# Four graph layers on one core: the last output stage written in place of the nodes' own term, with row scaling moved from GpSimd to VectorE in its second half

## The chip, the cores and the metric

The kernel runs on one core of a Trainium2 chip. The metric is device time in microseconds (us): the median of several runs of the whole program. A core has five engines that run their own instruction streams side by side and wait for each other by semaphores: PE (TensorE, matrix products), DVE (VectorE), ACT (ScalarE), POOL (GpSimd) and SP (SyncE, which here only issues DMAs). In the profile, a name with a q, such as SPq or POOLq, is the queue of that engine: what its sequencer handles itself.

## The reference, cut to what matters

Four layers on a graph of 4096 nodes with 128 features each. `x` is 4096x128 and `adj` a sparse 4096x4096 matrix, all in fp32. Each layer is added to its input and then normalized over the features:

```
x = _layernorm(x + _L0_gnn_ref(x, adj, adj, W, a))      # signed attention
x = _layernorm(x + _L1_gnn_ref(x, adj, W0, b0, W1, b1)) # Chebyshev, two steps
x = _layernorm(x + _L2_gnn_ref(x, adj, weight, ...))    # attention, 4 heads
x = _layernorm(x + _L3_gnn_ref(x, adj, W_self, W_neigh))
```

The change lies in the last layer, whose core is

```
deg = jnp.clip(jnp.sum(adj, axis=1, keepdims=True), 1.0)
h_neigh = adj @ h / deg
return h @ W_self + h_neigh @ W_neigh
```

with `h` the result of the third layer.

## The kernel before, in words

Nodes are cut into 32 tiles of 128 (`NT`), and into 8 blocks of 512 (`NB`, with `TB` = 4 tiles each). Layers 0 and 1 stream `adj` in chunks of 512x512. While they do, lists of each node's neighbours are built; with them layer 2 gathers single rows instead of multiplying whole matrices (`gathers`, `edges`, `sums`, `divide`). All this is built by `network(True)`. A flag, found while the lists are built, says whether they hold all neighbours; if not, the general `network(False)` runs after it. Both stand in one program: at line 1952 a conditional reads the flag, and each engine branches past the second network when it has done its part of the first. After that comes the end of the program (recorded at line 1983), where each engine drains and they meet in a barrier.

Layer 3 follows layer 2 tile by tile. `layer3_rows` keeps two things for each tile of nodes: `y`, its term for the neighbours, and `x[:, t, :]`, the nodes' own term (`h @ W_self` and the residual, scaled). A column of ones in `y` makes the same product yield the row sums of `adj`. `layer3_product` multiplies `y` with columns of `adj` and `add_up` adds the products into `acc3`, which lies transposed, features by nodes.

`layer3_end` closes one block of 512 nodes, and is a generator of three parts:

- Part 1. PE turns the block's columns of `acc3` upright with the help of the identity and adds the product of the last tile into the same PSUM buffer `p` (lines 1796 and 1798). DVE makes the reciprocal degrees (1800, 1801). It then forms, for each of four tiles, `p` times the reciprocal plus `x` into `o`, with the row sum beside it (1803). Line 1805 fills the last feature with minus that sum, so that each row has mean zero. DVE also takes the square sum of tile 3 (1807).
- Part 2. ACT takes the square sums of tiles 0 to 2 (1811) and the square root for all four (1812).
- Part 3. DVE makes the reciprocal (1814). ACT scales the rows of tiles 0 and 1 (1818), POOL those of tiles 2 and 3 (1820). SP stores the block, 256 KB (1821).

`o` has three buffers in the pool `l2`; `x` is one tile for all 4096 nodes that lives through the whole kernel. For PE, DVE, ACT and POOL the order of the instructions is the one in which they are written in `sparse_layers`. The loop at its end interleaves the blocks:

```
for ib in range(NB + 1):
    if ib < NB:
        ends.append(layer3_end(NT - 1, 1, ib, late[ib // TB][:, ib % TB]))
        next(ends[-1])                # part 1 of block ib
    if ib:
        next(ends.popleft(), None)    # part 3 of block ib - 1
    if ib < NB:
        next(ends[-1])                # part 2 of block ib
```

On DVE, therefore, the order is part 1 of block n, line 1814 of block n-1, part 1 of block n+1; on ACT the scalings of block n-1, then the squares and the root of block n.

Of the kernel before, what the change touches and what calls it, by code (L numbers as in the profile page):

```python
# [11 lines left out]
F32 = mybir.dt.float32  # L12
# [5 lines left out]
ALU = mybir.AluOpType  # L18
# [3 lines left out]
P = 128  # L22
IB = 512
TB = IB // P
# [21 lines left out]
def adj_resnorm_d4(ctx: ExitStack, tc: tile.TileContext, x_in, xT_in, adj, adjT, pairs, w0g, w0gT, a0, w1a, b1a,  # L46
# [7 lines left out]
    nc = tc.nc  # L54
    N, F = x_in.shape
    NT = N // P
    NB = N // IB
# [15 lines left out]
    x = state.tile([P, NT, F], F32, name="x")  # L73
# [1501 lines left out]
    def sparse_layers(enter, lists, w, h0T):  # L1575
        psum, ps_p, ps_x = [enter(name=n, bufs=b, space=PSUM) for n, b in (("ps_u", 2), ("ps_p", 4), ("ps_x", 2))]
        l2 = enter(name="l2", bufs=2)
# [210 lines left out]
        def layer3_end(t0, n, ib, a):  # L1788


            p = ps_p.tile([P, TB, F], F32, name="pp")
            o = l2.tile([P, TB, F], F32, name="o", bufs=3)
            s = small.tile([P, 2, TB], F32, name="less", bufs=3)
            for k in range(TB):
                at = slice(ib * IB + k * P, ib * IB + (k + 1) * P)
                nc.tensor.matmul(p[:, k, :], acc3[:, at], ident, start=True, stop=False)
                for r in range(n):
                    nc.tensor.matmul(p[:, k, :], a[:, r, k * P:(k + 1) * P], y[:, t0 + r, :], start=False, stop=r == n - 1)
            r = small.tile([P, TB], F32, name="rdeg")
            nc.vector.tensor_scalar_max(r, p[:, :, F - 1], 1.0)  # L1800
            nc.vector.reciprocal(r, r)
            for k in range(TB):
                nc.vector.scalar_tensor_tensor(o[:, k, 0:F - 1], p[:, k, 0:F - 1], r[:, k:k + 1], x[:, ib * TB + k, 0:F - 1],  # L1803
                                               op0=ALU.mult, op1=ALU.add, accum_out=s[:, 0, k:k + 1])
            nc.vector.tensor_scalar_mul(o[:, :, F - 1], s[:, 0, :], -1.0)  # L1805
            junk = [l2.tile([P, F], F32, name=f"z{k}") for k in range(2)]
            nc.vector.scalar_tensor_tensor(junk[1], o[:, 3, :], 1.0, o[:, 3, :], op0=ALU.mult, op1=ALU.mult,  # L1807
                                           accum_out=s[:, 1, 3:4])
            yield
            for k in range(3):  # L1810
                nc.scalar.activation(junk[0], o[:, k, :], AF.Square, accum_out=s[:, 1, k:k + 1])  # L1811
            nc.scalar.activation(s[:, 1, :], s[:, 1, :], AF.Sqrt, bias=eps, scale=1.0 / F)
            yield
            nc.vector.reciprocal(s[:, 1, :], s[:, 1, :])  # L1814
            for k in range(TB):
                scale = s[:, 1, k:k + 1]
                if k < 2:
                    nc.scalar.activation(o[:, k, :], o[:, k, :], AF.Copy, scale=scale)  # L1818
                else:
                    nc.gpsimd.tensor_scalar(o[:, k, :], o[:, k, :], scale, None, op0=ALU.mult)  # L1820
            nc.sync.dma_start(out[ib * IB:(ib + 1) * IB, :].rearrange("(k p) f -> p k f", p=P), o)

        with tc.manual_schedule(engines={mybir.EngineType.PE, mybir.EngineType.DVE, mybir.EngineType.Activation,
# [56 lines left out]
            for ib in range(NB):  # L1880
                if ib in LAST:
                    continue
                p = ps_p.tile([P, IB], F32, name="pp")
# [58 lines left out]
# [3 lines that stand above are left out]
                    next(ends[-1])  # L1945
                if ib:
                    next(ends.popleft(), None)
                if ib < NB:
                    next(ends[-1])
# [37 lines left out]
```

## Time and profile before

| what | value |
|---|---|
| runs | 1702.2, 1701.87 and 1694.86 us; median 1701.87 |
| profiled execution, its own time | 1874.19 us |
| its span, first to last instruction | 1872.1 us |
| busy share of the span | PE 84%, DVE 58%, ACT 20%, POOL 40% |
| granted TensorE clock, mean | 0.912 |
| output stage (layer3_end, 8 blocks) | 1831.4 to 1860.3 us of the span |
| busy in 1846.7 to 1860.3 | PE 0, DVE 6.18, ACT 9.04, POOL 5.91 us |
| busy in 1860.3 to 1872.1 | no engine |

The profile is of one execution, and its times count from the start of its span. The busy shares are means over stages with different limits, so a stage is read by itself: in which order its instructions start, and what ended the idle time ahead of each. Instructions that only move registers, branch, wait or drain are not counted as busy; where no engine is busy they are found under their line, on the queue of their engine.

### The profile page before, as it was taken

Reading aid. Unit: us, or ns where it says so; the run is one execution under the profiler, and the core shown is the slowest. Engines: PE = TensorE matmul, PEld = TensorE weight load, DVE = VectorE, ACT = ScalarE, POOL = GpSimd, SP = SyncE. Lnnn points to the kernel's source line nnn. Section 1 sums busy time; section 2 is a strip of 40 time slices with the busy share of each in tenths; the row PEclk is TensorE's granted clock in tenths of the full one; section 3 lists DMA queues with packets and bytes.
Section 4 is the critical chain, followed back from the end, with each engine's and each line's share of the span. In section 5 each row is a group of like instructions: output and inputs, shape, how many; then the busy total and the mean of one; then the engine's idle time right before and its main releaser. Section 6 shows DMA issues by size and latency. Waiting matters only on the chain. (4 is left out here: it accounts for less than half of the span.)

```text
span 1872.1 us, 16259 instructions
## 1 busy us (share of the span) xinstructions
PE 1565.8 (84%) x4804; PEld 748.6 (40%) x4808; DVE 1089.5 (58%) x3185; ACT 371.7 (20%) x681; POOL 742.0 (40%) x1142
## 2 busy tenths in 40 slices
PE   6999999999999789789898986849934668867784
PEld 3344445444444334334344443424422334433433
DVE  5655457988798485865686211424344645546564
ACT  4765400100001010102000000212222101112123
POOL 0000000000001718260687878870057776766732
PEclk9999999999999999899898998979957788888897
DMA  9887665688887375666686865727844465666572
GB/s 373 338 323 278 230 242 193 255 311 307 293 298 263 113 265 171 255 210 226 216 280 241 279 248 193 267 73 261 261 103 138 149 227 184 213 210 225 187 205 68
DMA packets 102601, 429.24 MB, mean 229 GB/s; under 512 B 20387, under 2 KB 38822, under 8 KB 60646
## 3 DMA queue, kind: packets, MB, share of 16 engines
q1 hardware_dynamic: 64400, 380.99, 57.1%
q0 software_dynamic: 20352, 31.44, 6.7%
q10 hardware_dynamic: 17750, 15.67, 2.6%
q8 instruction: 40, 0.66, 0.1%
q14 instruction: 59, 0.48, 0.1%
HBM read 416.43 MB, written 11.60 MB: 229 GB/s over the span
## 5 line engine op out<-in xcount | busy, mean ns | idle before, releaser
L1666 POOL DMA_INDIRECT got<-table,source x288 | 276.3, 959 | 188.7 <-DVE most L1507 115.5
L1773 PE MATMUL pp<-chunk,xT 128*128 128x512 f32 x496 | 257.5, 662 | 5.5 <-issue 5.2
L1439 POOL DMA_INDIRECT both_ways<-in_pairs,both_at x108 | 107.7, 997 | 359.1 <-DVE both_at L1421 307.4
L691 PE MATMUL pacc<-chunk,t 128*128 128x512 f32 x512 | 227.8, 599 | 5.1 <-issue 3.9
L1439 POOL DMA_INDIRECT got<-rows,source x180 | 180.9, 1005 | 114.9 <-issue 95.8
L691 PE MATMUL pacc<-chunk,x 128*128 128x512 f32 x512 | 222.0, 592 | 0.0
L1319 DVE MAX8 top<-chunk 128x8 f32<-128x512 f32 x224 | 144.6, 679 | 86.1 <-DMA chunk<-in_adjT 81.6
L397 PE MATMUL pacc<-chunk,hw 128*128 128x512 f32 x408 | 186.8, 602 | 0.3 <-DVE hw L440 0.2
L1887 PE MATMUL pp<-chunk,w 128*128 128x512 f32 x384 | 183.2, 627 | 3.3 <-issue 3.3
L1320 DVE FIND_INDEX8 at<-top,chunk 128x8 uint16<-128x512 f32 x224 | 151.3, 685 | 0.0
L691 PEld LDWEIGHTS pacc<-chunk,t 128*128 128x128 f32 x512 | 96.6, 192 | 121.7 <-issue 119.7
L691 PE MATMUL pacc<-chunk,v 128*128 128x512 f32 x320 | 145.1, 604 | 0.0
L691 PEld LDWEIGHTS pacc<-chunk,x 128*128 128x128 f32 x512 | 96.3, 190 | 116.2 <-issue 116.2
L1773 PEld LDWEIGHTS pp<-chunk,xT 128*128 128x128 f32 x496 | 99.4, 214 | 97.5 <-issue 94.6
L1286 POOL IOTA i<- 128x384 int32 (+3 forms) x4 | 1.0, 259 | 336.7 <-PE pden L385 323.5
L397 PEld LDWEIGHTS pacc<-chunk,hw 128*128 128x128 f32 x408 | 74.3, 190 | 90.5 <-issue 85.6
L1887 PEld LDWEIGHTS pp<-chunk,w 128*128 128x128 f32 x384 | 75.2, 203 | 88.0 <-issue 88.0
L328 DVE TENSOR_SCALAR pos<-chunk 128x2048 bf16<-128x2048 f32 x66 | 80.4, 1222 | 43.7 <-DMA chunk<-in_adjT 42.3
L369 ACT ACTIVATE junk<-chunk 128x2048 fp8e4<-128x2048 f32 x51 | 97.4, 1910 | 27.2 <-DMA chunk<-in_adjT 26.6
L1483 POOL TENSOR_TENSOR idle<-idle 128x1 f32<-128x1 f32 x417 | 93.7, 225 | 7.0
L1786 DVE TENSOR_TENSOR acc<-pp,acc 128x512 f32<-128x512 f32 x96 | 62.2, 683 | 58.0 <-PE pp L1773 29.2
L1476 DVE SCALAR_TENSOR_TENSOR here<-got,back,here 128x128 f32<-128x128 f32 x120 | 42.1, 351 | 87.4 <-DMA got<-rows,source 75.9
(349 smaller groups left out, 1894.2 us busy)
## 6 DMA issues: line engine op xcount, KB each, us to landing
chunk<-in_adjT SPq DMA_DIRECT2D x346, 1024.0 KB
keep<-in_adjT SPq DMA_DIRECT2D x13, 1024.0 KB
spread<-spread ACTq DMA_DIRECT2D x16, 384.0 KB
got<-table,source POOLq DMA_INDIRECT x288
got<-rows,source POOLq DMA_INDIRECT x180
table<-rows ACTq DMA_DIRECT2D x8, 264.0 KB
xT<-in_xT ACTq DMA_DIRECT2D x8, 256.0 KB
rows<-v ACTq DMA_DIRECT2D x8, 256.0 KB
```

Of the source, the lines that this page charges most:

```text
L328: r = nc.vector.tensor_scalar(pos, a, 0.0, None, op0=ALU.is_gt)
L369: nc.scalar.activation(junk, a, AF.Relu, scale=-1.0, accum_out=bad[:, n:n + 1], saturate=False)
L397: in_order(nc.tensor.matmul(p, hw[:, j * TB + k, :], a[:, k, :], start=first and k == 0, stop=last and k == TB - 1))
L691: nc.tensor.matmul(p, stationary(c * TB + k), a[:, k, :], start=n == 0 and k == 0, stop=n == NB - 1 and k == TB - 1)
L1319: nc.vector.max(self.top[:, t, ib, :], row)
L1320: nc.vector.max_index(self.at[:, t, ib, :], self.top[:, t, ib, :], row)
L1439: tc.keep_in_program_order(nc.gpsimd.indirect_dma_start(out, None, of, bass.IndirectOffsetOnAxis(ap=index, axis=0)))
L1483: return nc.gpsimd.tensor_tensor(self.idle[:, 0:1], of, self.idle[:, 1:2], ALU.mult)
L1666: nc.gpsimd.indirect_dma_start(got[t][:, j, :], None, table, bass.IndirectOffsetOnAxis(ap=lists.source[:, t, j:j + 1], axis=0))
L1773: nc.tensor.matmul(p, y[:, t0 + k, :], a[:, ib % (TB // n), k, :], start=k == 0, stop=k == n - 1)
L1786: nc.vector.tensor_add(acc3[:, blk], p, acc3[:, blk])
L1887: nc.tensor.matmul(p, w[:, c * TB + k, :], a[:, k, :], start=n == 0 and k == 0, stop=n == NB - 1 and k == TB - 1)
```

## The change

The tile `o` no longer has buffers of its own: it names the block's four tiles of `x`, and line 1803 reads the nodes' own term from the place that it writes. In blocks 0 to 3 POOL scales the rows of tiles 2 and 3 as before. In blocks 4 to 7 one DVE instruction scales both, with the two reciprocals spread over 128 elements each. ACT's share, the order of the parts and the store are unchanged in the text.

```
-            o = l2.tile([P, TB, F], F32, name="o", bufs=3)
+            o = x[:, ib * TB:(ib + 1) * TB, :]
...
             for k in range(TB):
-                nc.vector.scalar_tensor_tensor(o[:, k, 0:F - 1], p[:, k, 0:F - 1], r[:, k:k + 1], x[:, ib * TB + k, 0:F - 1],
+                nc.vector.scalar_tensor_tensor(o[:, k, 0:F - 1], p[:, k, 0:F - 1], r[:, k:k + 1], o[:, k, 0:F - 1],
                                                op0=ALU.mult, op1=ALU.add, accum_out=s[:, 0, k:k + 1])
...
                 if k < 2:
                     nc.scalar.activation(o[:, k, :], o[:, k, :], AF.Copy, scale=scale)
-                else:
+                elif ib < NB // 2:
                     nc.gpsimd.tensor_scalar(o[:, k, :], o[:, k, :], scale, None, op0=ALU.mult)
+            if ib >= NB // 2:
+                nc.vector.tensor_tensor(o[:, 2:4, :], o[:, 2:4, :], s[:, 1, 2:4][:, :, None].to_broadcast([P, 2, F]), ALU.mult)
             nc.sync.dma_start(out[ib * IB:(ib + 1) * IB, :].rearrange("(k p) f -> p k f", p=P), o)
```

## The prediction

> **What bounds the kernel now.** The page first: no engine is full over the span (PE 84%, DVE 58%, POOL 40%), but the diff touches only `layer3_end`, the output stage, so shares of the whole span decide nothing here. The windows view puts that stage at 1831.4 to 1860.3 of 1872.1 us, with nothing busy after it. Next I read its timeline by engine. The columns are start, duration, engine, line and what it does; in brackets stand the idle time before it and who ended it.
>
> ```profile
> 1840.61 0.18 DVE L1814 RECIPROCAL less<-less 128x4 f32<-128x4 f32 x1 [0.24 <-ACT less L1812]
> ...
> 1842.60 0.35 DVE L1803 SCALAR_TENSOR_TENSOR o<-pp,rdeg,x 128x127 f32<-128x127 f32 x1 [1.55 <-DMA out<-o]
> ...
> 1844.23 0.17 DVE L1814 RECIPROCAL less<-less 128x4 f32<-128x4 f32 x1
> ...
> 1848.17 0.35 DVE L1803 SCALAR_TENSOR_TENSOR o<-pp,rdeg,x 128x127 f32<-128x127 f32 x1 [1.08 <-POOL o L1820]
> ...
> 1851.25 0.35 DVE L1803 SCALAR_TENSOR_TENSOR o<-pp,rdeg,x 128x127 f32<-128x127 f32 x1 [1.02 <-DMA out<-o]
> ...
> 1854.31 0.35 DVE L1803 SCALAR_TENSOR_TENSOR o<-pp,rdeg,x 128x127 f32<-128x127 f32 x1 [0.99 <-DMA out<-o]
> ...
> 1858.36 0.18 DVE L1814 RECIPROCAL less<-less 128x4 f32<-128x4 f32 x1 [2.25 <-ACT less L1812]
> 1858.57 0.69 ACT L1818 ACTIVATE o<-o,less 128x128 f32<-128x128 f32 x2 [0.24 <-DVE less L1814]
> 1858.69 1.18 POOL L1820 TENSOR_SCALAR o<-o,less 128x128 f32<-128x128 f32 x2 [1.24 <-issue]
> ```
>
> Four times L1803 stands still because its buffer of `o` (three exist) has not been stored yet; the one put down to POOL (whose work on that buffer was done at 1845.68) ends 2.5 us after that block's store was issued, so it is a store too. The last block closes with POOL's two scalings, 0.6 us behind ScalarE's.
>
> Then the part with no busy engine, from the answers on the lines of the conditional (L1952) and of the end of the program (L1983). The columns are queue, operation and count, duration in ns (least/median/most), first and last start.
>
> ```profile
> L1952 POOLq COMPARE_BRANCH  x1: 57/57/57, 1859.4 to 1859.4; - x1
> L1952 SPq COMPARE_BRANCH  x1: 58/58/58, 1860.3 to 1860.3; - x1
> ...
> L1952 POOLq EVENT_SEMAPHORE  x1: 17/17/17, 1862.5 to 1862.5; - x1
> ...
> L1983 POOLq DRAIN  x3: 40/107/8734, 1862.5 to 1871.8; - x3
> L1983 SPq DRAIN  x3: 7/7/13, 1864.8 to 1871.5; - x3
> ```
>
> Of POOL's three drains the first begins at 1862.5 and must be the long one: the next POOL record is at 1871.3. SP is through its own work at 1864.8 and waits about 6.5 us for the barrier. **The span ends on POOL's drain**, 0.9 us after it. So two things bound the end: the output blocks' chain, and after it the engine that was used last.
>
> [...] so I read the 8.73 us as execution, not as a wait for SP. [...] POOL's next record comes 3.1 us after its branch (1859.4 to 1862.5). [...]
>
> **The change, part by part.** Starts of L1814, one per block: 1838.18, 1840.61, 1844.23, 1846.65, 1849.80, 1852.88, 1855.93, 1858.36. Undisturbed steps are 2.43 us: ScalarE's round of two scalings (0.60 until the next may start), three squares with accumulator reads (1.3), a square root (0.30), and the way over L1814 and back. The steps with a stall are 3.62, 3.15, 3.08 and 3.05, so the stalls cost 1.19 + 0.72 + 0.65 + 0.62 = 3.18 us.
>
> 1. *Output in place.* The buffer wait goes: a block of `x` is written once and stored once, and no later block reuses it. The instructions and their shapes stay. In-place output costs nothing: L1786 already adds in place at 683 ns mean, 692 in this window. All eight steps become 2.43 us: **-3.2 us**. Late next is ScalarE's round; the products are not, since PE ends at 1845.9, ahead of the last blocks.
> 2. *Blocks 4 to 7: two POOL instructions become one DVE instruction.* [...] L1632, 128x264, 432 ns at the median. It starts when L1814 is done, 0.21 us after that one's start, while L1800 now starts 0.09 after it. So L1800 and all of the next block's DVE work behind it move by 0.21 + 0.34 (424 ns less the overlap of about 0.08) - 0.09 = 0.46 us. DVE's round without waits is 2.10 us (1838.18 to the accumulator read at 1840.28); with the addition it is 2.56, or 0.13 more than ScalarE's. That counts in the steps after blocks 4 and 5; after 6 no next block stands behind: **+0.26 us**. [...] with twice the duration it is some 1.1 us.
> 3. *The close of block 7.* POOL ended 1.51 us after L1814's start (1859.87); DVE ends after 0.21 + 0.42 = 0.63 and ScalarE after 0.90 (1859.26). The last store can go 0.61 us sooner: **-0.6 us**. Its issue, landing and SP's branch stay as long; SP waits for one DVE and one ScalarE count in place of POOL's.
> 4. *POOL free early.* New L1814 of block 3: 1838.18 + 3 x 2.43 = 1845.47; POOL ends at +1.51, 1846.98. With the 2.6 us now between its last work and the drain, and 8.73 us of drain, it is done at 1858.3. SP, all parts above included (-3.18 + 0.26 - 0.61 = -3.5), is ready at 1864.8 - 3.5 = 1861.3, so the drain is covered by 3.0 us of other work. The end is now SP's arrival plus 0.9: 1862.2. If that cover were gone, up to 6.4 us would come back.
>
> Sum: 1862.2 against 1872.1, **-9.9 us**: -3.5 from the chain, -6.4 from the drain. No DMA is added and none is moved past another; the chunk loads stand ahead of the stores on SP as before. The dropped tile stands in its pool ahead of only `z0` and `z1`; I count that move at nothing.
>
> The profiled execution took 1874.19 us, 172 us more than the median of 1701.87 of the runs. These 9.9 us are latencies in a stage of small work, so I carry them over unscaled: 1701.87 - 9.9 = **1692.0 us**. Scaled by 1701.87/1874.19 they are 9.0. The drain was never seen apart from POOL's last work, nor outside a profile; its worth lies between 0 and 6.4 us, and I take the upper end [...]. The stalls are worth 0 to 3.2 us, since without the profile the stores may land sooner; a landing 1.2 us shorter would leave no stall.
>
> **The rivals.** About 0.5% (8.5 us) is what a measurement of this kernel can tell from no change; the three runs alone span 7.3 us.
>
> *The drain ends with the program, not with POOL's work.* If it waits for something late (the stores, or the last records of the other queues), POOL's freedom is worth nothing and only -3.5 remains: 1698.4 us, no change. For it speaks that the long one is the first and that the two later ones, all being quiet, take 107 and 40 ns; against it that the last store lands near 1862.9 and SP sees all landed by 1864.8, while the drain runs to 1871.2.
>
> *No stalls without the profile.* Then the blocks give 0.6 - 0.26 = 0.35 us and the drain 6.4: 1695.1 us, no change.
>
> *Slower: `x` is held as one.* If L1803 of block n+1 waited for the store of block n-1, since both touch `x`, every step would be POOL's close (1.51), the store (2.94 in the chain of waits), some 0.14 of handing over, and 1.63 from L1803 to L1814: 6.22 us, or 5.61 where DVE and ScalarE close. Four of the first, two of the second and a last 2.43 make 38.5 us against the 20.2 now: +18.3, less 0.6 and the drain's 6.4, or +11.3: 1713.2 us. It decides as soon as the distance of the waited-for store is two blocks where it was three buffers. Against it: ScalarE (1838.39) and POOL (1838.46) write different rows of one `o` at the same time, so rows are told apart.
>
> **How the numbers follow.** Forecast 0.60; drain tied to the end 0.15; no stalls 0.13; `x` as one 0.05; the rest (a move in the earlier layers that I don't see) 0.07, split evenly. The forecast lies only 1.4 us beyond the bound, and its unknown terms lean to less, so I count 0.85 of it as faster, and a quarter of the two rivals between: 0.51 + 0.07 = 0.58. Slower: 0.05 + 0.02. The range reaches from the forecast with both terms full and 5 us of the runs' spread below, 1687, to the drain rival and the spread above it, 1700.
>
> **What would show it.** In the changed profile: no L1803 with an idle time put down to a store; steps of L1814 of 2.43 us, some 2.56 late; a DVE instruction of 128x256 near 0.42 us four times; POOL's last record near 1847, its long drain from about 1849.6 and as long as now; SP's drain near 1861 and the end within 1 us of it. Wrong would be a POOL drain that still ends after SP's, or a wait at L1803 for a store.

## The result, and the profile after

The changed kernel takes 1689.58 us (median of 6 runs, 1687.68 to 1693.04), against 1700.46 us before (6 runs, 1694.86 to 1702.2). The ratio is 0.9942, with a 95% interval of 0.9924 to 0.996: about 10 us faster, as was forecast (1692.0).

The two profiled spans, 1872.11 and 1688.77 us, can't be subtracted. The one of before fell on an execution 172 us longer than the median, and nearly all of that was lost ahead of the output stage: the stage's first L1800 starts at 1833.44 us there and at 1659.76 after, 173.7 us apart, where no line was edited. From that instruction on the two traces can be compared: the steps that nothing disturbs are 2.43 us in both. It is 38.7 us from it to the end before and 29.0 after, **9.7 us less**.

The timeline of DVE and ACT after, for the output stage (start, duration, engine, line, what it does; in brackets the idle time before it and who ended it):

```profile
1667.46 0.35 DVE L1803 SCALAR_TENSOR_TENSOR x<-pp,rdeg,x 128x127 f32<-128x127 f32 x1
...
1669.35 0.18 DVE L1814 RECIPROCAL less<-less 128x4 f32<-128x4 f32 x1 [0.17 <-ACT less L1812]
...
1674.20 0.18 DVE L1814 RECIPROCAL less<-less 128x4 f32<-128x4 f32 x1 [0.17 <-ACT less L1812]
1674.41 0.42 DVE L1822 TENSOR_TENSOR x<-x,less 128x256 f32<-128x256 f32 x1
...
1677.00 0.17 DVE L1814 RECIPROCAL less<-less 128x4 f32<-128x4 f32 x1
...
1682.01 0.18 DVE L1814 RECIPROCAL less<-less 128x4 f32<-128x4 f32 x1 [1.79 <-ACT less L1812]
1682.22 0.42 DVE L1822 TENSOR_TENSOR x<-x,less 128x256 f32<-128x256 f32 x1
1682.22 0.69 ACT L1818 ACTIVATE x<-x,less 128x128 f32<-128x128 f32 x2 [0.24 <-DVE less L1814]
```

L1803 no longer has a bracket: no block waits for a store. Where L1814 has one, it waits for ACT's square root; at 1677.00 it has none, because DVE's own round is the longer one there. The eight L1814 start at 1664.49, 1666.92, 1669.35, 1671.78, 1674.20, 1677.00, 1679.59 and 1682.01: four steps of 2.43 us, then 2.80, 2.59 and 2.42.

The lines of the conditional (now L1954) and of the end of the program (now L1985), after (queue, operation, count, duration in ns least/median/most, first and last start):

```profile
L1954 POOLq COMPARE_BRANCH  x1: 57/57/57, 1672.7 to 1672.7; - x1
...
L1954 POOLq EVENT_SEMAPHORE  x1: 17/17/17, 1675.4 to 1675.4; - x1
...
L1954 SPq COMPARE_BRANCH  x1: 57/57/57, 1683.4 to 1683.4; - x1
...
L1985 POOLq DRAIN  x3: 40/107/8734, 1675.5 to 1688.5; - x3
L1985 SPq DRAIN  x3: 7/7/13, 1687.9 to 1688.2; - x3
```

The long drain is as long as before, to the nanosecond, but it begins at 1675.5 and so is over at 1684.2, ahead of the drains of ACT (1685.7) and DVE (1686.0). SP arrives at 1687.9 and the span ends 0.9 us later. The waits of SP say the same: at the end it stood 7.2 us for the other queues before and 0.7 after (us in total, times, longest; first before, then after).

```profile
SPq L1983 <- PEq L1983: 7.2, 2, 6.7
```

```profile
SPq L1985 <- PEq L1985: 0.7, 2, 0.5
```

The view names PE, but PE's own drain was done at 1848.2 before and at 1675.0 after, so it was not PE that came last. Before, it was POOL: its long drain ends at 1871.3, and SP's next record is at 1871.5.

### The profile page after: what moved, and what is told of

The parts are those of the page before. It is cut to its first block, busy times and chain, and to the rows that moved or that the text cites. A ratio compares the mean times of both kernels' runs of the same rounds, so it can differ in the third digit from the quotient of the medians.

```text
span 1688.8 us, 16243 instructions
## 1 busy us (share of the span) xinstructions
PE 1519.6 (90%) x4808; PEld 731.8 (43%) x4808; DVE 1089.2 (64%) x3189; ACT 371.7 (22%) x681; POOL 740.8 (44%) x1134
## 4 chain that ended last, share of the span: by engine, by line
PE 51%; DVE 16%; POOL 13%; issue 9%; DMA 7%; ACT 3%; ACTq 0%; DVEq 0%; POOLq 0%
PE pacc L691 21%; PE pacc L397 13%; POOL got L1439 6%; POOL got L1666 5%; PE pp L1889 4%; DMA got<-table,source 4%; PE pp L1773 3%; DVE at L1320 2%; DVE top L1319 2%; POOL idle L1483 2%; DMA chunk<-in_adjT 2%; DVE gw L1702 1%; DVE acc L1786 1%; PE pden L385 1%; PE ptr L340 1%
## 5 line engine op out<-in xcount | busy, mean ns | idle before, releaser
L1773 PE MATMUL pp<-chunk,xT 128*128 128x512 f32 x496 | 243.5, 632 | 1.6 <-ACT xT L1748 0.7
L1889 PE MATMUL pp<-chunk,w 128*128 128x512 f32 x384 | 170.2, 593 | 0.0
L1773 PEld LDWEIGHTS pp<-chunk,xT 128*128 128x128 f32 x496 | 94.2, 203 | 90.8 <-issue 83.9
L1889 PEld LDWEIGHTS pp<-chunk,w 128*128 128x128 f32 x384 | 70.6, 190 | 76.4 <-issue 76.4
L691 PEld LDWEIGHTS pacc<-chunk,v 128*128 128x128 f32 x320 | 60.3, 192 | 79.0 <-issue 79.0
```

Source lines behind the costliest of these rows:

```text
L691: nc.tensor.matmul(p, stationary(c * TB + k), a[:, k, :], start=n == 0 and k == 0, stop=n == NB - 1 and k == TB - 1)
L1773: nc.tensor.matmul(p, y[:, t0 + k, :], a[:, ib % (TB // n), k, :], start=k == 0, stop=k == n - 1)
L1889: nc.tensor.matmul(p, w[:, c * TB + k, :], a[:, k, :], start=n == 0 and k == 0, stop=n == NB - 1 and k == TB - 1)
```

## The experiments

All ratios are to the kernel before, on the same chip as the run. The edits are shown against the full change. The stage is measured within each profile, from the first L1814 to the end of the span; it was 33.94 us before and 24.27 with the full change.

**E1: output in place, GpSimd scales in all blocks.**

```
-                elif ib < NB // 2:
+                else:
...
-            if ib >= NB // 2:
-                nc.vector.tensor_tensor(...)
```

> Output in place, but GpSimd scales in all eight blocks. Theory (two separate gains: no store is waited for, and GpSimd's 8.73 us drain is covered): the chain loses its stalls, 3.2 us, and the drain still follows the last block's scaling, so the end stays 6.4 us behind SP's arrival: 3.2 us below the kernel before, about 1697.3 us; steps of L1814 all 2.43 us. Rival (no stalls outside a slow profile): within 0.5 us of before. Rival (the whole gain comes from in-place output): some 10.9 us below before, like the full change.

Measured: ratio 0.9979 (0.9969 to 0.9989), 3.6 us below 1697.74. In its profile all seven steps of L1814 are 2.42 to 2.43 us and the stage takes 30.7 us, 3.2 less than before. Its lines of the end:

```profile
L1983 POOLq DRAIN  x3: 40/107/8734, 1676.4 to 1685.6; - x3
L1983 SPq DRAIN  x3: 7/7/13, 1678.6 to 1685.4; - x3
```

SP is ready at 1678.6 and POOL's drain ends at 1685.1: the whole gap of 6.5 us is still there. Both rivals fall: the stalls exist in timed runs too, and in-place output alone brings a third of the gain.

**E2: VectorE scales in blocks 4 to 7, `o` keeps its three buffers.**

```
-            o = x[:, ib * TB:(ib + 1) * TB, :]
+            o = l2.tile([P, TB, F], F32, name="o", bufs=3)
...
-  ... r[:, k:k + 1], o[:, k, 0:F - 1], ...
+  ... r[:, k:k + 1], x[:, ib * TB + k, 0:F - 1], ...
```

> Three buffers of o as before, but VectorE scales in blocks 4 to 7. Theory: the stalls stay (the store of block 4 goes 0.6 us earlier, so the last stall shrinks by that), the close gains 0.6 us, and the drain is covered, 6.4 us: about 7.6 us below before, near 1692.9 us; GpSimd's long drain ends some 4 us ahead of SP's. Rival (the drain ends with the program): at most 1.2 us below before.

Measured: ratio 0.9965 (0.9951 to 0.9978), 5.9 us. The stage takes 27.5 us, 6.5 less than before, where 7.6 was expected. The timeline of its DVE shows the stalls again:

```profile
1667.43 0.35 DVE L1803 SCALAR_TENSOR_TENSOR o<-pp,rdeg,x 128x127 f32<-128x127 f32 x1 [1.93 <-DMA out<-o]
...
1673.00 0.35 DVE L1803 SCALAR_TENSOR_TENSOR o<-pp,rdeg,x 128x127 f32<-128x127 f32 x1 [1.08 <-POOL o L1820]
...
1676.52 0.35 DVE L1803 SCALAR_TENSOR_TENSOR o<-pp,rdeg,x 128x127 f32<-128x127 f32 x1 [0.98 <-DMA out<-o]
```

Three stalls instead of four (the one put down to POOL is a store too, as before): the last is gone, since the store of block 4 had landed 1.4 us before block 7 needed its buffer. But two of the others are longer than expected, and the chain of waits shows why (start, duration, what):

```profile
1664.13 3.17 DMA out<-o
...
1673.02 3.38 DMA out<-o
```

The stores of blocks 0 and 3 landed 3.17 and 3.38 us after they were issued, against 2.80 and 2.94 in the profile of before, and L1803 starts 0.12 us after each landing, as it did there. The new DVE instruction of block 4 was thus hidden in the stall behind the store of block 3. From the first to the last L1814 it is 20.67 us, not the 19.6 that the expectation amounts to: 0.8 us of the excess are the two later landings, 0.15 is the step after the last stall (2.58 us), where the DVE instruction does show, and another 0.15 is a late start of the second L1803 in block 6 that also stands in the full change. What delays a landing is not shown. The close (0.6 us) and the drain came as expected, and the rival falls: it allowed at most 1.2 us, and the interval begins at 3.7. The lines of the end:

```profile
L1985 POOLq DRAIN  x3: 40/107/8734, 1675.2 to 1689.8; - x3
L1985 SPq DRAIN  x3: 7/7/13, 1689.2 to 1689.5; - x3
```

POOL's drain is over at 1683.9, well before SP's arrival. The two halves of the change add up: 3.2 and 6.5 make 9.7. That they meet so closely is in part chance: the last stall is gone in both, and E2's late landings took 0.8 us away.

**E3: the full change, and one small GpSimd instruction at the very end.**

```
+            if ib == NB - 1:
+                nc.gpsimd.tensor_scalar(lists.idle[:, 1:2], s[:, 1, 0:1], 1.0, None, op0=ALU.mult)
```

> The full change plus one GpSimd instruction of 128x1 that waits for the last block's reciprocal, L1814; nobody waits for its result. Theory (the drain follows GpSimd's last work and takes 8.73 us whatever that work is): its drain starts near the program's end again, SP's arrival is unchanged, and the span grows by 6.5 to 6.9 us over the full change: about 1696.2 us. Rival (the drain's cost comes with the eight scalings that were dropped, or it is tied to the end of the program): no difference from the full change.

Measured: ratio 0.9972 (0.9963 to 0.9982), 4.7 us below before, so much of the gain is lost. The stage takes 30.9 us, 6.6 more than with the full change. The timeline of POOL, then the lines of the end:

```profile
1670.57 1.19 POOL L1820 TENSOR_SCALAR x<-x,less 128x128 f32<-128x128 f32 x2 [1.24 <-DVE rdeg L1800]
1680.86 0.38 POOL L1825 TENSOR_SCALAR idle<-less 128x1 f32<-128x1 f32 x1 [9.11 <-DVE less L1814]
```

```profile
L1987 POOLq DRAIN  x3: 40/107/8734, 1684.3 to 1693.6; - x3
L1987 SPq DRAIN  x3: 7/7/13, 1686.4 to 1693.3; - x3
```

An instruction of 0.38 us whose result nobody needs costs 6.6 us: POOL's branch (1681.4) and its long drain (1684.3 to 1693.0) now come after it. SP is ready as soon as in the full change (23.4 us after the first L1814 in both). The drain follows POOL's last work, 3.1 us after its end here, 2.2 in the full change and 2.9 in E6; it goes neither with the number of scalings nor with the end of the program. It costs time in the runs as well: the interval of this kernel, 3.1 to 6.3 us below before, lies apart from that of the full change, 6.8 to 12.9.

**E4: in place, GpSimd scales in blocks 0 to 6.**

```
-                elif ib < NB // 2:
+                elif ib < 7:
...
-            if ib >= NB // 2:
+            if ib >= 7:
```

> In place, GpSimd scales in blocks 0 to 6, VectorE only in block 7. Theory: the chain is 0.5 us shorter than in the full change (no VectorE addition between two blocks), but GpSimd's last scaling starts near 4.9 us later relative to the stage than SP allows for: its drain ends about 3.9 us after SP is ready, and the span is 3.4 us longer than in the full change, near 1693 us. Rival (any block in which GpSimd rests at the end is enough): 0.5 us below the full change.

Measured: ratio 0.9964 (0.995 to 0.9978), 6.1 us. The stage takes 28.0 us, 3.7 more than the full change (3.4 expected).

```profile
L1985 POOLq DRAIN  x3: 40/107/8734, 1676.1 to 1685.3; - x3
L1985 SPq DRAIN  x3: 7/7/13, 1680.5 to 1685.1; - x3
```

The drain ends at 1684.8, 4.2 us after SP is ready. One block of rest covers a part of it; the rest of the 8.73 us shows.

**E5: the full change again**, in one comparison with E6 to E8.

> The full change once more, on the chip of the runs beside it. Theory: 9.6 us below before, as the stage is 9.6 us shorter in its profile (33.9 to 24.3 us from the first L1814 to the end), so about 0.994 of before; the four single edits (-3.2, -6.4 and the rest) were measured on another chip than the full change, and this gives it a comparison of its own. Rival (part of the first 10.9 us was the chip or the day): clearly less, about 7 us.

Measured: ratio 0.995 (0.9935 to 0.9965), 8.5 us below 1696.57; its stage takes 24.2 us. The first and the second comparison agree within their intervals, and both hold the 9.7 us of the traces. Whether a part of the first 10.9 us between medians was the chip can't be told at this width.

**E6: in place, GpSimd scales in no block.**

```
-                elif ib < NB // 2:
+                elif ib < 0:
...
-            if ib >= NB // 2:
+            if ib >= 0:
```

> In place, VectorE scales tiles 2 and 3 in all eight blocks, GpSimd in none. Theory: GpSimd's drain is covered already in the full change, so its freedom from the gathers on is worth nothing more; VectorE's round of 2.57 us now sets all steps of L1814 in place of ScalarE's 2.43, so the span from the first L1814 to the end grows by some 0.3 us against the full change. The long drain follows gathers here instead of scalings; if it is 8.73 us again, it does not depend on the kind of work before it. Rival (less GpSimd is always better): shorter than the full change.

Measured: ratio 0.9953 (0.9936 to 0.997), not told apart from E5. In the profile six steps of L1814 are 2.57 to 2.58 us and the last 2.42, and the stage takes 24.6 us, 0.4 more than E5.

```profile
L1985 POOLq DRAIN  x3: 44/107/8730, 1630.6 to 1684.6; - x3
```

After gathers and their small filler instructions the drain is 8730 ns, against 8734 after scalings, so the kind of work before it makes no difference here. It ends 45.6 us ahead of the span's end, so the record is no wait for the other queues. With it covered, more freedom for GpSimd brought nothing.

**E7: the full change without the last Exp table load.**

```
-            nc.scalar.activation(warm, eps, AF.Exp)
+            if t0 + n < NT:
+                nc.scalar.activation(warm, eps, AF.Exp)
```

> The full change, and the last call of layer3_rows no longer brings back the Exp table with its dummy activation, which nobody needs after it. Theory: in the output stage the table load of 1.28 us at L1812 in block 0 stands between ScalarE's squares and the first square root, so it is on the path to every later L1814: 1.3 us below the full change. Rival (the first block waits for something else): no difference.

Measured: ratio 0.9945 (0.993 to 0.996), against 0.995 for E5: not told apart. In the profile the table load before the first square root is gone, but from the first L1800 to the end it is 28.3 us against 29.0 with the full change (28.9 in E5): 0.6 to 0.7 us, half of what was expected. The timeline of ACT and DVE, whose line numbers are one higher, shows why:

```profile
1659.59 0.30 ACT L1813 ACTIVATE less<-less,eps 128x4 f32<-128x4 f32 x1
...
1660.32 0.29 DVE L1808 SCALAR_TENSOR_TENSOR z<-x 128x128 f32<-128x128 f32 x1
1660.54 0.08 DVE L1808 DVE_READ_ACCUMULATOR z<-x 128x1 f32 x1
1660.54 0.17 DVE L1815 RECIPROCAL less<-less 128x4 f32<-128x4 f32 x1
```

The root is there at 1659.9, but the reciprocal stands on DVE behind part 1 of block 1 until 1660.54. The table load covered that work; half of it came back as DVE's.

**E8: a version for the best time**, with E7's edit, GpSimd in blocks 0 to 4, and the last store on ScalarE's queue.

```
-                elif ib < NB // 2:
+                elif ib < 5:
...
-            nc.sync.dma_start(out[...], o)
+            (nc.scalar if ib == NB - 1 else nc.sync).dma_start(out[...], o)
```

> A version for the best time: the full change without the last Exp table load, GpSimd scaling in blocks 0 to 4 (its drain then ends about 1.3 us ahead of SP), and the last block's store issued by ScalarE's queue, so that SP branches while that store is still being made. Theory: 1.3 us for the table, 0.4 for one VectorE addition less between blocks, 0.5 to 0.9 for SP, together some 2.3 us below the full change. Rival (the drain or ScalarE's branch behind its store becomes the last): no better than the table load alone.

Measured: 1685.57 us, ratio 0.994 (0.9922 to 0.9958), the lowest median of all, yet not told apart from E5 or E7 by the runs. From the first L1800 to the end it is 27.5 us, 1.4 less than E5 (2.3 expected): 0.65 from the table, 0.3 from the steps of L1814, and the rest at the end.

```profile
L1986 POOLq DRAIN  x3: 40/107/8734, 1674.7 to 1684.0; - x3
L1986 SPq DRAIN  x3: 7/7/13, 1683.4 to 1683.7; - x3
```

SP comes 22.6 us after the first reciprocal, and POOL's drain, expected 1.3 us ahead of it, now ends at 1683.4 as well: the cover is used up. Letting GpSimd do a fifth block and getting SP through sooner pulled at the same margin.

All ten profiles together, in us from the first reciprocal of row norms (L1814 or its shifted line); SP is ready when its first drain starts, the end of POOL's drain is its start plus 8.73, and a negative time lies ahead of that reciprocal:

| kernel | SP ready | POOL's drain ends | end of the span |
|---|---|---|---|
| before | 26.6 | 33.1 | 33.9 |
| after | 23.4 | 19.7 | 24.3 |
| E1 in place only | 23.4 | 29.9 | 30.7 |
| E2 scaling only | 26.6 | 21.3 | 27.5 |
| E3 late GpSimd | 23.4 | 30.0 | 30.9 |
| E4 GpSimd in seven | 22.9 | 27.2 | 28.0 |
| E5 after, again | 23.3 | 19.6 | 24.2 |
| E6 GpSimd in none | 23.7 | -21.0 | 24.6 |
| E7 no table load | 23.3 | 19.8 | 24.2 |
| E8 best | 22.6 | 22.6 | 23.4 |

In every row the last column is the later of the other two plus 0.8 or 0.9 us. In-place output moves the first of them, the split of the scaling the second.

## Why the prediction was right

1. *No stall behind a store: -3.2 us.* E1 does this alone and gives 3.2 us in the trace and 3.6 (1.9 to 5.3) in the runs. The prediction speaks of eight steps; between eight starts lie seven, and its sum is right. Writing in place left L1803 as long as it was: 347 ns at the median before and after.
2. *The added VectorE instruction: +0.26 us.* It takes 424 to 425 ns. The 424 of the prediction can be had as an estimate from the trace of before: L1718, a TENSOR_TENSOR of 128x128, takes 292 ns at the median there and L1632, 128x264, 432, and a line through the two gives 424 at 128x256. E6 shows DVE's round at 2.57 to 2.58 us against the 2.56 predicted. The two steps in question are 2.80 and 2.59 in the full change, so the term is 0.53, twice the predicted one. Most of the excess lies in block 6: its second L1803 starts 0.42 us after the first where 0.27 is usual, and ahead of the first DVE's queue handles a semaphore that E6 does not have at that place, and L1803 starts 0.07 us later. E3 and E2 have the same 0.15 us at the same instruction, so it is not POOL's drain (in E3 that begins 10 us later); E6, where other instructions stand ahead, has none. What it is stays open.
3. *The close of block 7: -0.6 us.* The store waits for ACT, which ends 0.90 us after the start of L1814 as predicted. From the last L1814 until SP is ready it is 5.9 us, 6.4 before: 0.5 of the 0.6 us arrive.
4. *The drain covered: -6.4 us.* The step with the largest unknown held. That the drain's record is no wait for SP was an assumption, and E6 bears it out: its 8730 ns end 45.6 us ahead of the end of the span. The runs settle it from both sides: with GpSimd's last work late (E1, E3), the 6.5 us are there, and with it early (the full change, E2) they are not. The prediction had a margin of 3.0 us between the drain and SP; it is 3.7: the drain begins 2.2 us after POOL's last work where 2.6 had been taken from before, and SP is ready 0.3 us later than predicted.

The sum is 9.7 us in the traces against 9.9. One more thing in the text was less sound than its result. The profile's own time was noted as 172 us too long without asking where: that it was lost ahead of the stage is what made the unscaled sum right, and the prediction did not know it.

Of the rivals, "the drain ends with the program" fell with E3 and with the after profile, "no stalls without the profile" with E1. "`x` is held as one" would have shown a bracket on each L1803, and there is none.

## What to carry to other kernels

Read the stretch after the last busy instruction too: list each queue's records on the last lines, find which queue arrives last at the barrier, and ask when it could have been released. GpSimd had a long way out here, 8.73 us of drain: giving it its last work early saved 6.5 us for 0.53 us more on VectorE, and giving it no scaling at all (E6) saved nothing further, since its way out was covered already. ScalarE and VectorE fed each other in rounds here, and taking time from one gave back no more than the distance to the other: E7 freed 1.28 us on ScalarE and kept 0.6 to 0.7.

## What the runs showed that I had not expected

GpSimd's first drain at the end took 8730 to 8734 ns in all ten profiles, whether scalings, one 128x1 instruction or gathers came before it; its next two took some 0.1 and 0.04 us. What it does in that time is not shown. SP has a way out of its own: in the kernels before and after it stood 3.1 us between its branch and its next record. With the last store on ScalarE's queue (E8) it branched 7.3 us ahead of the end of the span, where it was 5.4 after, but then stood 5.0 us, so less than it had gained in starting earlier came out at the end. The landings in the traces tell why. In E8 the last part of that store lands at 1681.99 us and SP's next record starts at 1682.01: it stood for the store. Before and after, the last store had landed 0.8 and 0.6 us ahead of that record, so there SP's own way out was the longer one. From the last L1814 until SP is ready it is 5.4 us in E8 and 5.8 in E5.
